# First attention of a hybrid block: sums alone in a group's first step, heads and outputs copied out of PSUM by ScalarE, the shared expert's gate and up apart, dense work in other steps

## The chip, the core and the metric

The kernel runs on one core of a Trainium2 chip. The metric is the device time of one execution in microseconds (us), from the runs of the kernel; lower is better. Five engines work side by side, each through its own queue in order: PE (TensorE, matmuls into PSUM), DVE (VectorE), ACT (ScalarE), POOL (GpSimd) and SP (SyncE, which issues most DMAs). They wait for each other through semaphores.

## The reference, cut to what matters

The program runs four layers over 16 sequences of 512 tokens of width 256, that is 8192 tokens: a softmax attention, a mixture of experts, an attention with forget gates, and the mixture of experts once more. The change touches the first attention and the part of the first mixture of experts that runs beside it.

```python
x = x + attn_a(layernorm(x))                     # 16 heads of 16, rope on q and k
x = x + ffn(layernorm(x))                        # 64 experts, top 8, and a shared expert
...
# attn_a
q, k, v = proj(Wq), proj(Wk), proj(Wv)
scores = einsum('bhqd,bhkd->bhqk', rope(q), rope(k)) / sqrt(16)
out = einsum('bhqk,bhkd->bhqd', softmax(scores), v)
return out.reshape(B, S, D) @ Wo.T
...
# shared expert, in ffn (192 wide)
gu = x @ ws_gate_up
shared = silu(gu[:, :192]) * gu[:, 192:] @ ws_down
```

## The kernel before, in words

All is in fp32. The first attention works in **blocks** of 512 tokens (one sequence, `nblk` = 16), each block in four **groups** of four heads, each group in four **steps** of 128 tokens. A block thus has 16 steps, and the loop over `s` runs from 32 steps ahead of block 0 to the end of block 15. The order of every engine's queue but POOL's is the order in which the loop calls the work (`manual_schedule`); `each(s)` yields it, so the tables in it are the schedule.

In a step, for group n and its i-th 128 tokens:

- `weighted(n, i)` (L364): four matmuls (L329, one per head, side by side on four row strips of PE) give the scores of 128 keys against 512 queries, and ACT takes four exponents (L369). `largest(n + 2, i)` (L338): four matmuls of the same kind (also L329) for the group two ahead, of which DVE takes the row maxima with four reduces (L343). The profile calls both L329; each matmul shows as two instructions. This is "L329" or "the scoring" in what follows.
- In step 0 of a group: `summed(n - 1)` (L373), 16 matmuls (L379, two instructions each) that sum the weighted values of the group before, copied out by ACT (L144); then `turn(n + 3)` of the keys (L312), four transposes (L318) and an ACT copy.
- In step 1: `heads(n - 1)` (L388, calls `heads_out`), four transposes (L152) of which DVE takes a reciprocal and a product straight from PSUM (L156, L160) into `ao`; `row(n + 1)` (L347), which brings the maxima into a row of the turned queries through PE, ACT (L359) and four SP DMAs (L362); then `turn(n + 3)` of the queries.

Behind that a step calls what the tables `dense` and `routed` (L423, L438) hold for its place in the block. The second number of an entry is how many blocks away the work belongs (`queries, 1` is for the next block, `output, -1` for the last one). `load`, `moments`, `normed`, `features` (L232 to L250) bring a block in, normalise it on DVE and turn it (L225); `queries` (L252, L255) projects queries and keys and leaves the rope to POOL; `values` (L295, L299); `joined` turns `ao` (L395); `output` (L398) multiplies by Wo (L402), and DVE adds it to `x` straight from PSUM (L409). `part.*` is the first mixture of experts, two or three blocks behind: `part.shared(b, piece)` runs the shared expert's up to three 128-wide chunks of gate and up (L1605) and its silu (tanh on ACT, L991, and two DVE products, L992 and L993, that read PSUM), `part.down` its second matmul (L1636); `part.moments`, `part.normed`, `part.features`, `part.logits`, `part.likely`, `part.exps`, `part.choose`, `part.count` and `part.added` make the router's tokens (L1516 turns them), logits (L1525), probabilities (L1537, L1539), choices and counts. `part.shared` and `part.down` are left out for the last blocks and done behind the loop.

Every matmul result takes one of eight PSUM banks, `bank()` (L214), in the order of the calls and in turn: a new result waits until whatever was read from the bank eight calls ago has been read. A step takes four banks for `weighted`, four for `largest`, and one for each further result (two for eight transposes).

Of the kernel before, what the change touches and what calls it, by code (L numbers as in the profile page):

```python
# [9 lines left out]
F32 = mybir.dt.float32  # L10
U32 = mybir.dt.uint32
AF = mybir.ActivationFunctionType
ALU = mybir.AluOpType
# [4 lines left out]
P = 128  # L18
D = 256
KD = D // P  # L20
H = 16
HD = D // H
HP = 32
NHG = 4
BLK = 512
# [12 lines left out]
class Block:  # L38
# [105 lines left out]
        self.nc.scalar.copy(oT, pav)  # L144
        return oT

    def heads_out(self, out, oT, hg, bank, den_eps=None):

        nc = self.nc
        pt = bank()  # L150
        for c in range(CB):
            nc.tensor.transpose(pt[:, ts(c, P)], oT[:, ts(c, P)], self.ident)  # L152
        o = pt.rearrange("p (c j k) -> p c j k", j=NHG, k=HP)
        rec = self.small.tile([P, CB, NHG], F32, name="rec")
        if den_eps is None:
            nc.vector.reciprocal(rec, o[:, :, :, HD])  # L156
        else:
            nc.vector.tensor_scalar(rec, o[:, :, :, HD], den_eps, None, ALU.add)
            nc.vector.reciprocal(rec, rec)
        nc.vector.tensor_tensor(  # L160
            out[:, :, ts(hg, NHG * HD)].rearrange("p c (j d) -> p c j d", d=HD),
            o[:, :, :, 0:HD],
            rec.unsqueeze(3).to_broadcast([P, CB, NHG, HD]),
            ALU.mult,
        )


    def attention(self, x, x1, wqkv, wo, rope, part, later):

# [9 lines left out]
        nc, tc = self.nc, self.tc  # L179
        with ExitStack() as c:  # L180
# [6 lines left out]
            p2 = c.enter_context(tc.tile_pool(name="a_2", bufs=2, side="left"))  # L187
# [200 lines left out]
            def heads(n):  # L388
                b, hg = divmod(n, NHG)
                if hg == 0:  # L390
                    aos[b] = p1.tile([P, CB, D], F32, name="ao")
                self.heads_out(aos[b], oTs.pop(n), hg, bank)


            def joined(b):  # L395
# [2 lines left out]
            def output(b, i):  # L398
                po = bank()
                for k in range(2):  # L400
                    for kd in range(KD):
                        nc.tensor.matmul(  # L402
                            po[:, ts(k, D)],
                            lhsT=aoTs[b][:, kd, ts(i + k, P)],
                            rhs=wo_sb[:, kd, :],
                            start=(kd == 0),
                            stop=(kd == KD - 1),
                        )
                nc.vector.tensor_tensor(  # L409
                    xs[b][:, i : i + 2, :],  # L410
                    xs[b][:, i : i + 2, :],
                    po.rearrange("p (c d) -> p c d", c=2),
                    ALU.add,
                )
# [6 lines left out]


            dense = {  # L423
                0: [(load, 2)],
                2: [(queries, 1, 2)],
                3: [(part.shared, -2, 1), (queries, 1, 3)],
                4: [(joined, -1)],
                6: [(values, 1, 0)],
                7: [(values, 1, 2)],
                8: [(moments, 2)],  # L430
                9: [(normed, 2)],
                10: [(output, -1, 0)],
                11: [(output, -1, 2)],
                13: [(features, 2)],
                14: [(queries, 2, 0)],
                15: [(queries, 2, 1)],
            }
            routed = {  # L438
                0: [(part.added, -3)],
                1: [(part.shared, -2, 0)],  # L440
                4: [(part.choose, -2, 0), (part.choose, -2, 1)],
                5: [(part.down, -2, 0), (part.choose, -2, 2)],
                9: [(part.down, -2, 2)],
                12: [(lambda b: part.moments(b, xs[b]), -1)],
                13: [(part.count, -2), (lambda b: part.normed(b, xs.pop(b)), -1)],
                14: [(part.features, -1)],
                15: [(part.logits, -1), (part.likely, -1), (part.exps, -1)],
            }
            steps, groups, z = NHG * CB, self.nblk * NHG, self.nblk - 1

            def each(s):

                n, i = divmod(s, CB)
                yield groups, n, weighted, i
                yield groups, n + 2, largest, i
                if i == 0:
                    yield groups, n - 1, summed
                    yield groups, n + 3, turn, kTs, H, "kT"
                if i == 1:
                    yield groups, n - 1, heads  # L460
                    yield groups, n + 1, row
                    yield groups, n + 3, turn, qTs, 0, "qT"
                b, at = divmod(s, steps)
                for work, far, *args in dense.get(at, []) + routed.get(at, []):

                    if b + far < z - 2 or work not in (part.shared, part.down):
                        yield self.nblk, b + far, work, *args

            with tc.manual_schedule(
                engines={  # L470
# [903 lines left out]
class Part:  # L1374
# [6 lines left out]
    def __init__(self, ctx, k, x, y, weights, room, pairs, side):  # L1381
# [21 lines left out]
            self.hTs,  # L1403
            self.ys,
            self.gus,
        ) = [{} for _ in range(12)]
        self.end = 0.0
        self.bank = None
        self.shared_weights = (rw, ws_gu, ws_down)
# [187 lines left out]


    def gu(self, b, piece):
        nc, xnT = self.nc, self.xnTs[b]  # L1600
        gu = self.gus[b, piece] = {}
        for m in ((0, 2), (1,))[piece]:
            gu[m] = self.bank()
            for kd in range(KD):
                nc.tensor.matmul(  # L1605
                    gu[m],
                    lhsT=self.wsg_sb[:, kd, ts(m, P)],
                    rhs=xnT[:, kd, :],
                    start=(kd == 0),
                    stop=(kd == KD - 1),  # L1610
                )
        if piece == 1:
            del self.xnTs[b]

    def silu(self, b, piece):
# [7 lines left out]
        self.k.silu(self.hTs[b][0:high, piece, :], gate, up, th, 0.5)  # L1623

    def shared(self, b, piece):
        self.gu(b, piece)
        self.silu(b, piece)
# [137 lines left out]
```

## Time and profile before

| | |
|---|---|
| median of 3 runs | 2688.24 us (2686.0 to 2689.28) |
| the profiled execution's own time | 2689.83 us |
| its span, first to last instruction | 2688.0 us |
| mean granted clock of PE | 0.953 |
| PE, DVE, ACT, POOL busy over the span | 91%, 71%, 48%, 31% |
| last heads of the first attention (L160, last start) | 1374.4 us |
| granted clock 107 to 119 and 119 to 125 us | 0.76 and 0.63 |
| granted clock 200 to 1200 us | 1.00 |
| granted clock 1299 to 1309 us | 0.56 |

How to read it: the span holds all four layers one after the other; what is said of one of them has to be read in its own stretch. Matmuls are pipelined and their ends are modelled, so PE's busy share says little; where a stretch of the chain of waits lies on PE from end to end, the length of each of its pieces is what counts, and a piece that is longer than its like elsewhere stood still on a wait.

### The profile page before, as it was taken

To read this page: it belongs to the slowest core of one execution; us is meant where nothing else is said; L and a number is where in the kernel's file an instruction comes from. 1 tells how busy PE (TensorE), PEld (TensorE's weight loads), DVE (VectorE), ACT (ScalarE), POOL (GpSimd) and SP (SyncE) were. 2 spreads that over 40 slices of the span, in tenths; PEclk is the share of its full clock that TensorE was granted. 3 is DMA by queue.
4 is the path that set the end of the run, shared out by engine and by line. 5 is a ranking of instruction groups with operands and counts; after the bars stand their busy time and mean duration, and the time that the engine had idled before them with its cause. 6 is when DMAs were issued, how large, how long until landed. Compare 5 with 4: busy or idle time off the path is not lost.

```text
span 2688.0 us, 47635 instructions
## 1 busy us (share of the span) xinstructions
PE 2447.6 (91%) x17864; PEld 1511.5 (56%) x17864; DVE 1895.4 (71%) x4646; ACT 1291.3 (48%) x2654; POOL 844.7 (31%) x804
## 2 busy tenths in 40 slices
PE   7999999999999999999988885899999969998781
PEld 3445455545455544555446775567667656667671
DVE  6666667666677666776646664899999869967650
ACT  1656556565566655665532332455555523323330
POOL 3122222122221222212015775332232122127773
PEclk7999999999999999999898998999999969999996
DMA  1000111001110001100158986201111058739987
GB/s 57 2 17 19 35 37 35 21 22 35 35 35 21 29 29 35 36 19 21 40 133 234 239 223 145 69 29 60 56 52 53 21 145 184 176 106 262 239 217 147
DMA packets 210003, 226.48 MB, mean 84 GB/s; under 512 B 34286, under 2 KB 202222, under 8 KB 208750
## 3 DMA queue, kind: packets, MB, share of 16 engines
q1 hardware_dynamic: 180366, 174.43, 22.5%
q0 software_dynamic: 25728, 46.15, 8.9%
q8 instruction: 143, 2.34, 0.4%
q10 hardware_dynamic: 3680, 2.85, 0.3%
q14 instruction: 86, 0.70, 0.1%
HBM read 146.50 MB, written 84.48 MB: 86 GB/s over the span
## 4 chain that ended last, share of the span: by engine, by line
PE 68%; DVE 15%; DMA 9%; issue 3%; POOL 1%; ACT 1%; SPq 0%; ACTq 0%; POOLq 0%; DVEq 0%
PE sc L329 20%; PE sc L379 9%; DMA xe<-rows,token 6%; PE sc L255 4%; DVE pT L841 4%; PE sc L1605 3%; PE sc L318 3%; DVE qkT L805 2%; PE sc L299 2%; PE sc L402 2%; PE sc L1636 2%; PE pb L792 2%; PE pb L717 2%; PE sc L1137 2%; PE sc L824 1%
## 5 line engine op out<-in xcount | busy, mean ns | idle before, releaser
L343 DVE TENSOR_REDUCE mx<-sc 128x1 f32<-128x512 f32 x1024 | 635.2, 682 | 375.7 <-PE sc L329 375.6
L369 ACT ACTIVATE pT<-sc 128x512 f32<-128x512 f32 x1024 | 528.6, 602 | 179.5 <-PE sc L329 179.5
L329 PE MATMUL sc<-qT,kT 17*128 17x512 f32 x2048 | 315.6, 646 | 0.0
L329 PE MATMUL sc<-kT,qT 16*128 16x512 f32 x2048 | 312.4, 609 | 1.5 <-DVE mx L343 1.4
L104 POOL TENSOR_SCALAR va<-mv 128x4 f32<-128x4 f32 x64 | 14.7, 230 | 797.1 <-DVE mv L98 797.1
L379 PE MATMUL sc<-pT,v 128*32 128x512 f32 x2048 | 241.8, 614 | 0.0
L329 PEld LDWEIGHTS sc<-kT,qT 16*128 16x128 f32 x2048 | 159.6, 189 | 94.4 <-issue 52.1
L841 DVE SCALAR_TENSOR_TENSOR pT<-sc,of,left 128x256 f32<-128x256 f32 x512 | 204.6, 472 | 4.3 <-PE sc L824 4.3
L277 POOL TENSOR_TENSOR t<-qk,rope_sb 128x512 f32<-128x512 f32 x62 | 78.8, 1270 | 403.4 <-ACT qk L263 396.6
L1107 POOL DMA_INDIRECT xe<-rows,token x128 | 128.5, 1004 | 96.2 <-DVE token L1089 39.0
L379 PEld LDWEIGHTS sc<-pT,v 128*32 128x32 f32 x2048 | 61.3, 112 | 173.1 <-issue 123.0
L329 PEld LDWEIGHTS sc<-qT,kT 17*128 17x128 f32 x2048 | 93.8, 184 | 89.9 <-issue 46.1
L255 PE MATMUL sc<-wqkv_sb,feat 128*128 128x512 f32 x256 | 127.4, 623 | 0.0
L144 ACT COPY oT<-sc 128x512 f32<-128x512 f32 x64 | 37.6, 587 | 169.4 <-PE sc L379 169.4
L792 PE MATMUL pb<-feat,wqk_sb 128*128 128x512 f32 x256 | 117.7, 593 | 0.0
L1172 POOL DMA_INDIRECT routed<-ye,token x64 | 105.0, 1641 | 39.1 <-DMA routed<-ye,token 16.2
L96 DVE BATCH_NORM_STATS2 bn<-x 128x6 f32<-128x256 f32 x256 | 89.0, 410 | 17.7 <-DMA x<-out 12.9
L318 PEld LDWEIGHTS sc<-ident,pad 128*128 128x128 f32 x512 | 54.8, 142 | 74.1 <-issue 38.9
L805 DVE SCALAR_TENSOR_TENSOR qkT<-ez,rz 128x512 f32<-128x512 f32 x64 | 93.9, 1487 | 0.0
L318 PE MATMUL sc<-ident,pad 128*128 128x128 f32 x512 | 86.1, 291 | 5.2 <-POOL pad L293 3.0
L285 POOL TENSOR_TENSOR t<-qk,rope_sb 128x256 f32<-128x256 f32 x124 | 90.7, 753 | 0.0
L1605 PE MATMUL sc<-xnT,wsg_sb 128*128 128x512 f32 x192 | 89.3, 603 | 0.0
(218 smaller groups left out, 4807.0 us busy)
## 6 DMA issues: line engine op xcount, KB each, us to landing
ws<-in_w_gate SPq DMA_DIRECT2D x64, 384.0 KB
ws<-in_w_up SPq DMA_DIRECT2D x64, 384.0 KB
rows<-xn SPq DMA_DIRECT2D x32, 512.0 KB
routed<-y SPq DMA_DIRECT2D x32, 512.0 KB
ws<-in_w_down SPq DMA_DIRECT2D x64, 256.0 KB
x<-in_x SPq DMA_DIRECT2D x16, 512.0 KB
attended<-x SPq DMA_DIRECT2D x16, 512.0 KB
ws<-in_w_down SPq DMA_DIRECT2D x64, 128.0 KB
```

The source lines that it names most:

```text
L255: nc.tensor.matmul(pq, lhsT=xnTs[b][:, kd, ts(i, P)], rhs=wqkv_sb[:, kd, 0 : 2 * D], start=(kd == 0), stop=(kd == KD - 1),)
L318: nc.tensor.transpose(pt[:, ts(i, P)], pads[b % 2][i][:, at : at + 4, :].rearrange("p h d -> p (h d)"), self.ident,)
L329: nc.tensor.matmul(scs[j], lhsT=lhs[at : at + high, ts(i, P)], rhs=rhs[at : at + high, :], start=True, stop=True,)
L343: nc.vector.tensor_reduce(mxs[n][:, j, i : i + 1], sc, AX.X, ALU.max, negate=True)
L369: nc.scalar.activation(pT[:, j, :], sc, AF.Exp, scale=float(HD) ** -0.5)
L379: nc.tensor.matmul(pav[ts(j, HP), :], lhsT=vs[b % 2][:, i, 4 * hg + j, :], rhs=pT[:, j, :], start=(i == 0), stop=(i == CB - 1),)
L792: nc.tensor.matmul(pq, lhsT=wqk_sb[:, kd, ts(m, P)], rhs=xnTs[b][:, kd, :], start=(kd == 0), stop=(kd == KD - 1),)
L805: nc.vector.scalar_tensor_tensor(qks[b][:, m, :], ez, 1.0, rz, ALU.min, ALU.add)
L841: nc.vector.scalar_tensor_tensor(pTs[n][:, :, ts(s8, HD)], sc[:, :, ts(s8, HD)], of[:, s8 : s8 + 1], here, ALU.mult, ALU.mult,)
L1107: nc.gpsimd.indirect_dma_start(out=xes[e], out_offset=None, in_=rows, in_offset=bass.IndirectOffsetOnAxis(ap=token[:, e : e + 1], axis=0),)
L1172: nc.gpsimd.indirect_dma_start(out=accs[e % 2], out_offset=bass.IndirectOffsetOnAxis(ap=token[:, e : e + 1], axis=0), in_=ye, in_offset=No ...
L1605: nc.tensor.matmul(gu[m], lhsT=self.wsg_sb[:, kd, ts(m, P)], rhs=xnT[:, kd, :], start=(kd == 0), stop=(kd == KD - 1),)
```

## The change

`heads_out` and `output` get a buffer `there`: ACT copies the PSUM result into it, and DVE works from there. The two tables become one, with its entries in other steps. `part.shared(-2, 0)`, which ran gate and up in one step, becomes `part.gate` (step 1) and `part.up` (step 3). In `each`, step 0 of a group calls the sums and no turn; the turn of the keys moves to step 1, ahead of the first dense entry, which itself comes ahead of `heads` and `row`; the turn of the queries moves to step 2. The copy in `heads_out` and `output` is also in what runs behind the loop.

```diff
-    def heads_out(self, out, oT, hg, bank, den_eps=None):
+    def heads_out(self, out, oT, hg, bank, pool, den_eps=None):
...
-        o = pt.rearrange("p (c j k) -> p c j k", j=NHG, k=HP)
+        there = pool.tile([P, BLK], F32, name="there")
+        nc.scalar.copy(there, pt)
+        o = there.rearrange("p (c j k) -> p c j k", j=NHG, k=HP)
...
-                self.heads_out(aos[b], oTs.pop(n), hg, bank)
+                self.heads_out(aos[b], oTs.pop(n), hg, bank, p2)
...
+                there = p2.tile([P, BLK], F32, name="there")
+                nc.scalar.copy(there, po)
                 nc.vector.tensor_tensor(
                     xs[b][:, i : i + 2, :],
                     xs[b][:, i : i + 2, :],
-                    po.rearrange("p (c d) -> p c d", c=2),
+                    there.rearrange("p (c d) -> p c d", c=2),
                     ALU.add,
                 )
...
             dense = {
-                0: [(load, 2)],
+                0: [(load, 2), (part.added, -3)],
+                1: [(part.gate, -2)],
                 2: [(queries, 1, 2)],
-                3: [(part.shared, -2, 1), (queries, 1, 3)],
-                4: [(joined, -1)],
-                6: [(values, 1, 0)],
-                7: [(values, 1, 2)],
+                3: [(part.up, -2), (queries, 1, 3)],
+                4: [(part.choose, -2, 0), (part.choose, -2, 1)],
+                5: [(part.shared, -2, 1), (joined, -1)],
+                6: [(values, 1, 0), (part.choose, -2, 2)],
+                7: [(part.down, -2, 0)],
                 8: [(moments, 2)],
-                9: [(normed, 2)],
-                10: [(output, -1, 0)],
-                11: [(output, -1, 2)],
-                13: [(features, 2)],
-                14: [(queries, 2, 0)],
-                15: [(queries, 2, 1)],
+                9: [(values, 1, 2), (normed, 2)],
+                10: [(output, -1, 0), (part.count, -2)],
+                11: [(features, 2), (output, -1, 2)],
+                12: [(lambda b: part.moments(b, xs[b]), -1)],
+                13: [(queries, 2, 0), (lambda b: part.normed(b, xs.pop(b)), -1)],
+                14: [(part.features, -1), (part.down, -2, 2)],
+                15: [(part.logits, -1), (part.likely, -1), (part.exps, -1), (queries, 2, 1)],
             }
-            routed = {
-                0: [(part.added, -3)],
-                1: [(part.shared, -2, 0)],
-                4: [(part.choose, -2, 0), (part.choose, -2, 1)],
-                5: [(part.down, -2, 0), (part.choose, -2, 2)],
-                9: [(part.down, -2, 2)],
-                12: [(lambda b: part.moments(b, xs[b]), -1)],
-                13: [(part.count, -2), (lambda b: part.normed(b, xs.pop(b)), -1)],
-                14: [(part.features, -1)],
-                15: [(part.logits, -1), (part.likely, -1), (part.exps, -1)],
-            }
+            expert = part.gate, part.up, part.shared, part.down
...
                 yield groups, n, weighted, i
                 yield groups, n + 2, largest, i
+                b, at = divmod(s, steps)
+                now = [
+                    (self.nblk, b + far, work, *args)
+                    for work, far, *args in dense[at]
+                    if b + far < z - 2 or work not in expert
+                ]
                 if i == 0:
                     yield groups, n - 1, summed
+                if i == 1:
                     yield groups, n + 3, turn, kTs, H, "kT"
-                if i == 1:
+                    yield from now[0:1]
                     yield groups, n - 1, heads
                     yield groups, n + 1, row
+                    now = now[1:]
+                if i == 2:
                     yield groups, n + 3, turn, qTs, 0, "qT"
-                b, at = divmod(s, steps)
-                for work, far, *args in dense.get(at, []) + routed.get(at, []):
-                    if b + far < z - 2 or work not in (part.shared, part.down):
-                        yield self.nblk, b + far, work, *args
+                yield from now
...
+    def gate(self, b):
+        gu = self.bank()
+        self.chunk(b, 0, gu)
+        self.hTs[b] = self.hidden[b % len(self.hidden)]
+        th = self.ths[b] = self.tile("th", [P, BLK])
+        self.nc.scalar.activation(th, gu, AF.Tanh, scale=0.5)
+        self.nc.vector.scalar_tensor_tensor(th, th, 1.0, gu, ALU.add, ALU.mult)
+
+    def up(self, b):
+        gu = self.bank()
+        self.chunk(b, 2, gu)
+        self.nc.vector.scalar_tensor_tensor(
+            self.hTs[b][:, 0, :], self.ths.pop(b), 0.5, gu, ALU.mult, ALU.mult
+        )
```

`chunk(b, m, to)` is the loop over two matmuls that `gu` had before, with the bank given to it.

More of the change, by code (lines that the diff above doesn't have):

```diff
@@ L1405, in __init__ @@
             self.gus,
-        ) = [{} for _ in range(12)]
+            self.ths,
+        ) = [{} for _ in range(13)]
         self.end = 0.0
@@ L1599, in gu @@
     def gu(self, b, piece):
-        nc, xnT = self.nc, self.xnTs[b]
         gu = self.gus[b, piece] = {}
@@ L1603, in gu, with chunk @@
             gu[m] = self.bank()
[L1604 to L1611, printed above, removed]
+            self.chunk(b, m, gu[m])
         if piece == 1:
             del self.xnTs[b]
+    def chunk(self, b, m, to):
+        for kd in range(KD):
+            self.nc.tensor.matmul(
+                to,
+                lhsT=self.wsg_sb[:, kd, ts(m, P)],
+                rhs=self.xnTs[b][:, kd, :],
+                start=(kd == 0),
+                stop=(kd == KD - 1),
+            )
     def silu(self, b, piece):
@@ L1623, in silu @@
         self.k.silu(self.hTs[b][0:high, piece, :], gate, up, th, 0.5)
+    def gate(self, b):
[10 more added lines that the diff above has]
+            self.hTs[b][:, 0, :], self.ths.pop(b), 0.5, gu, ALU.mult, ALU.mult
+        )
     def shared(self, b, piece):
```

## The prediction

> **What bounds the kernel now.** I read the page first, then the busy times of one block of the first attention, then the chain of waits there, then its timeline.
>
> ```profile
> PE 2447.6 (91%) x17864; PEld 1511.5 (56%) x17864; DVE 1895.4 (71%) x4646; ACT 1291.3 (48%) x2654; POOL 844.7 (31%) x804
> PE 68%; DVE 15%; DMA 9%; issue 3%; POOL 1%; ACT 1%; SPq 0%; ACTq 0%; POOLq 0%; DVEq 0%
> ```
>
> The whole kernel hangs mostly on PE, but that is an average over stages. The change touches only the stage up to about 1370 us (the last heads of the first attention). One of its blocks, by the view of stretches:
>
> ```profile
> 521.31:604.91 83.60, 83.60 (x562) 42.31 (x561) 57.96 (x129) 49.93 (x99) 19.63 (x22) 1.00 0.10 31
> ```
>
> A block lasts 83.60 us. PE's 83.60 means little, as ends of matmuls are modelled; what counts is that DVE (57.96) and ACT (49.93) have room, and that the chain there is PE alone. So only two things can be won: time in which PE's queue stands on a wait, and the cost of changing from one kind of matmul to another. Both show in the chain's pieces (start, length, what):
>
> ```profile
> 519.38 1.93 PE sc L329 x16
> 521.31 1.92 PE sc L402 x8
> 523.23 2.34 PE sc L329 x15
> 525.58 1.93 PE sc L402 x8
> ...
> 538.33 2.42 PE sc L329 x15
> 540.74 1.91 PE sc L255 x4
> ...
> 549.13 2.16 PE sc L329 x16
> 551.29 3.57 PE sc L379 x32
> 554.86 0.59 PE sc L318 x4
> ...
> 566.20 1.93 PE sc L329 x16
> 568.13 1.91 PE sc L1605 x4
> 570.05 1.72 PE sc L255 x4
> ```
>
> L329 is the scoring that opens every step, 1.93 us. Three of the sixteen in a block are longer: by 0.41 (step 11), 0.49 (step 14) and 0.23 (the next block's step 0). That is **1.13 us of waiting per block**. The last two lines show the other thing: four matmuls of 512 columns take 1.91 behind L329 and 1.72 behind matmuls of their own kind. Who is waited for, from the timeline:
>
> ```profile
> 523.73 0.68 DVE L409 TENSOR_TENSOR x<-x,sc 128x512 f32<-128x512 f32 x1
> 524.13 1.45 PE L329 MATMUL sc<-kT,qT 16*128 16x512 f32 x8
> ...
> 538.22 0.42 DVE L160 TENSOR_TENSOR ao<-sc,rec 128x256 f32<-128x256 f32 x1
> 538.26 1.20 PE L329 MATMUL sc<-qT,kT 17*128 17x512 f32 x7
> ```
>
> The eight PSUM banks are handed out in turn, so a step that takes d banks beyond its eight for L329 gives its positions d to d+7 to the next step's L329. DVE's add L409, queued behind four reduces, held the output's bank to 524.41; the second half of L329 (1.04 long elsewhere) took 1.45. L160 held the heads' bank to 538.64 likewise. The third, 0.23, is L1539, which reads the router's logits until 550.05.
>
> **The change, part by part, for a full block.** Times inside a step count from its L329's start: L329 ends at 1.93; ACT's four exponents run 1.2 to 3.3, DVE's four reduces 2.02 to 4.50, starting 0.60 apart (timeline: L329 at 519.31, L369 at 520.53, L343 at 521.33).
>
> *Copies out of PSUM.* Four heads and two outputs a block get an ACT copy, priced by the same copy in the second attention:
>
> ```profile
> L877 ACT COPY there<-pb 128x512 f32<-128x512 f32 x64 | 37.0, 578 | 0.3 <-PE pb L874 0.3
> L884 DVE TENSOR_TENSOR ao<-there,rec 128x256 f32<-128x256 f32 x64 | 27.2, 425 | 2.2
> L160 DVE TENSOR_TENSOR ao<-sc,rec 128x256 f32<-128x256 f32 x53 | 22.5, 424 | 1.8
> ```
>
> Six times 0.58 is 3.5 us of ACT; 49.9 becomes 53.4 of 83.6, hidden under PE. If ACT had no room it would be up to 3.5 a block. DVE's own time does not fall (425 against 424 ns), but the banks come free when ACT is done, 0.6 to 0.7 us behind PE, and no longer when DVE gets to them: the 0.41 and 0.49 go. [...]
>
> *Logits ahead of queries in step 15.* L1537 and L1539 then run right behind the reduces and end at about 5.3, a whole L329 before their bank is due (5.5 + 0.96): the 0.23 goes. All **1.13 is removed**.
>
> *Changes of kind.* Adding the chain's pieces (L329 1.93, sums 3.57, turn 0.59, heads 0.59, row 0.32, eight transposes 0.87, count 0.44, dense work 1.9 behind L329 and 1.72 to 1.80 behind others, logits 1.73) in the old order gives 82.4, with 1.13 of waits 83.55, which is the measured block. In the new order the steps come to: 0, 4, 8, 12 (sums alone) 5.50 each; 1, 5, 9, 13: 5.17, 6.04, 5.23, 5.15; 2, 6, 10, 14: 4.24, 4.32, 4.76, 5.19; 3, 7, 11, 15: 5.56, 3.85, 4.70, 5.48; together 81.7. So **0.73 less**, because eight dense pieces stood behind L329 and now four do. One change of kind is not in the trace: sums straight into L329. I give it the 0.1 that other changes cost (inside the 3.57). The nearest rows bound it: at nothing it saves another 0.4 a block; with a whole weight load of L329 uncovered on top (row of PEld: 185 ns) it costs 0.7 more.
>
> *New waits.* Here I walk the banks for each step; three places fail.
> (a) Step 5 takes six banks, so step 6's fourth L329 bank is that of the shared expert's third chunk. The chunk ends at 1.93 + 0.59 + 1.74 = 4.26, tanh (L991, 591 ns) starts 0.2 behind it as at 570.08 and ends at 5.05, DVE's L992 and L993 (680 and 690 ns) at 6.49; step 6 starts at 6.04: **0.45**.
> (b) Step 9: heads now stand behind a turn and the values. Their matmuls end at 4.9, their copy, behind that of the values, at 5.6; DVE's reciprocal starts there, and from it to the end of the normalising the old order took 2.58 (518.53 to 521.11): 8.2, that is 3.0 into step 10, where the reduces want DVE at 2.0. The third of them ends at 4.85 and its bank is due at 4.76: with a hand-over of 0.1, **0.2**.
> (c) Step 13 likewise: the router's normalised tokens are done, chunk by chunk, from 2.1 to 3.1 into step 14, where their transposes are due from 2.52 on: **0.4**. Before, queries stood between.
> Two others come within 0.1 (gate's bank in step 2, queries' in step 0); I add 0.05. New: **1.1**; each may be nothing, or twice that.
>
> The turns moved off step 0 are read two steps later, with their copy long done. The row's DMAs keep some 14 us to the next group, and SP's other issues (stores at steps 0, 6, 11, 13, 14) wait for nothing that would hold a row's. Heads of the first group now come ahead of "joined" on PE; the product waits for it on DVE, and DVE is then still at L993: nothing.
>
> *Sum.* 0.73 + 1.13 − 1.1 = 0.76 a block; 12 full blocks (2 to 13): **−9.1**. Blocks 0 and 1 lack the dense work of older blocks; L329 stretches to 11.44 for three steps at 107 us, and the sums behind it take 5.95 in place of 3.57 at a granted clock of 0.63 (119 to 125 us). Values and features now lie among these steps: **−3**, bounds 0 and −6. In block 15 (1299 to 1309 us, clock 0.56) work is missing in both orders: 0, bounds ±4. [...] Behind the loop, the last heads and the second output each get a copy in a chain that nothing covers (heads' product 1374.43, outputs 1378.36 and 1379.56): **+1.2**. The DMA-bound experts behind only shift. In all −10.9 against the profiled 2689.83 (span 2688.0); that execution lies 1.6 above the runs' median of 2688.24, so I forecast **2677**.
>
> **Rivals.** 1, *the new waits take all* (each of (a) to (c) 0.25 larger, or the sums' change of kind with its uncovered load): 0.0 to 0.1 a block, 2685 to 2688. For it: three waits went, three came. Against: the removed ones are measured, the new ones reckoned with latencies at their high end.
> 2, *DVE runs late, slower than before.* In steps 9 and 13 the queue copy, heads, normalising, reduces is serial; every us that the heads' copy comes later than 5.6 delays reduces and transposes at both places. From 0.4 us at each the gain of a block is gone; at 1.1 us each it costs 2.2 − 0.76 = 1.4 a block, 17 us, less 2 at the ends: 2703. For it: DVE already has 58 of 84 us, and its queue is in order. Against: ACT is free at that point (its turn's copy ends at 3.9).
> 3, *the new waits do not arise*: 1.9 a block, 22 us, with the ends 2664.
> 4, *no difference at all*, as PE is busy 83.60 of 83.60: 2688. Against: the three longer L329.
>
> **How the numbers follow.** Forecast 0.40, rival 3 0.16, rival 1 (with 4) 0.24, rival 2 0.20. A measurement here tells about 0.2% (5.4 us) from no change. Faster takes the forecast and rival 3: 0.56; the same 0.24; slower 0.20. The range runs from rival 3 with the half clocks gone (2661) to where half of rival 2 lies inside (2698). The forecast's own range is 2670 to 2683.
>
> **What would show it.** In the new profile a full block should last 82.8 us. No L329 is long behind an output or heads; those of steps 6 and 11 are long by 0.45 and 0.2, waiting for the shared expert's last product and for a reduce; the router's transposes in step 14 take 1.3 in place of 0.87. L329 right behind sums stays at 1.93. I am wrong if the block is over 83.6, or if L343 in steps 10 and 14 starts over 3.5 into its step.

## The result, and the profile after

The changed kernel takes **2717.74 us** (median of 4 runs, 2711.4 to 2720.38); the kernel before, beside it on the same chip, 2687.12 (4 runs, 2680.82 to 2689.28). The ratio is 1.0114, 95% interval 1.0088 to 1.014: 30 us slower, where 11 faster was forecast. The profiled execution took 2720.38, with a span of 2718.2.

The lines of code move a little: scoring is L334 (was L329), its reduces L348 (L343), sums L384, turn L323, queries L260, the rope's three lines L282, L290 and L298, the router's transposes L1523, its logits L1532, the shared expert's gate and up L1617, its second matmul L1662 ("down" below). New is L154, the heads' copy; behind it come L158 and L162, reciprocal and product.

Busy times and the shares of the chain of waits, from the page of the changed kernel:

```profile
PE 2454.6 (90%) x17864; PEld 1528.9 (56%) x17864; DVE 1930.3 (71%) x4646; ACT 1335.3 (49%) x2750; POOL 847.6 (31%) x804
PE 67%; DVE 17%; DMA 9%; issue 3%; ACT 1%; POOL 1%; SPq 0%; ACTq 0%; POOLq 0%; DVEq 0%
```

ACT has the 96 copies more. DVE issues exactly as many instructions as before (x4646) and yet is busy 35 us longer: some of the same instructions take more time. One block, by the view of stretches (length, busy time of PE, PEld, DVE, ACT, POOL, then the granted clock):

```profile
482.88:568.21 85.33, 83.36 (x565) 43.10 (x564) 60.58 (x129) 52.84 (x105) 19.83 (x22) 0.98 0.10 29
```

The block lasts 85.33 us, not 83.60 as before or 82.8 as forecast. PE is no longer busy from end to end, the granted clock is below 1.00, and DVE is busy 2.6 us longer with its 129 instructions. The chain of waits shows where (step 13 begins at 548.47, step 14 at 553.39, step 15 at 562.58; the last line is step 6 of the next block):

```profile
538.12 2.10 PE sc L334 x16
...
548.47 1.93 PE sc L334 x16
550.40 0.58 PE sc L323 x4
550.98 1.73 PE sc L260 x4
...
553.30 0.58 ACT there L154
...
553.90 0.26 DVE rec L158
...
554.19 0.81 DVE ao L162
555.00 0.63 DVE t L113
...
555.66 0.67 DVE t L114
...
556.55 1.26 DVE xn L122
557.81 0.14 issue
557.94 2.21 PE sc L1523 x8
560.15 2.43 PE sc L1662 x8
562.58 1.93 PE sc L334 x16
...
600.07 1.93 PE sc L334 x16
```

The pieces on PE have the lengths that their like have elsewhere, but for step 14 and 0.17 in step 11 (538.12). There the chain leaves PE: the router's transposes (L1523) wait for the normalising, and most of the DVE operations ahead of it are long. The product takes 0.81 (0.42 before), the two operations on 128 x 4 numbers 0.63 and 0.67 (0.15 and 0.16 before), the first normalised chunk 1.26 (0.41 before); together they are some 2.25 us longer. These are the short ones, in the timeline of before (the product's 0.42 stands in the prediction):

```profile
538.56 0.15 DVE L113 SCALAR_TENSOR_TENSOR t<-y 128x4 f32<-128x4 f32 x1
538.75 0.16 DVE L114 TENSOR_TENSOR t<-t,va 128x4 f32<-128x4 f32 x1
...
539.14 1.38 DVE L122 TENSOR_SCALAR xn<-x,mv,rstd 128x256 f32<-128x256 f32 x4
```

The timeline of the changed kernel shows what else runs:

```profile
553.46 1.26 POOL L282 TENSOR_TENSOR t<-qk,rope_sb 128x512 f32<-128x512 f32 x1 [3.03 <-ACT qk L268]
...
553.90 0.25 DVE L158 RECIPROCAL rec<-there 128x16 f32<-128x16 f32 x1 [1.00 <-ACT there L154]
...
554.19 0.81 DVE L162 TENSOR_TENSOR ao<-there,rec 128x256 f32<-128x256 f32 x1
...
554.68 1.62 POOL L290 TENSOR_TENSOR t<-qk,rope_sb 128x256 f32<-128x256 f32 x2
554.92 0.70 DVE L113 SCALAR_TENSOR_TENSOR t<-y 128x4 f32<-128x4 f32 x1
...
555.66 0.66 DVE L114 TENSOR_TENSOR t<-t,va 128x4 f32<-128x4 f32 x1
556.35 0.16 DVE L116 SCALAR_TENSOR_TENSOR rstd<-t,y 128x4 f32<-128x4 f32 x1
556.38 1.27 POOL L298 TENSOR_TENSOR pad<-t,t 128x512 f32<-128x512 f32 x1
...
556.55 2.21 DVE L122 TENSOR_SCALAR xn<-x,mv,rstd 128x256 f32<-128x256 f32 x4
...
557.94 2.21 PE L1523 MATMUL sc<-ident,xn 128*128 128x128 f32 x8 [1.97 <-DVE xn L122]
```

POOL's rope of the moved queries has four operations, ending at 554.72, 555.60, 556.30 and 557.64. The four long DVE operations end at 555.00, 555.62, 556.32 and 557.80: each 0.02 to 0.28 behind the end of one on POOL. L116 starts just before the last of them and takes its 0.16; the three chunks after the rope take 0.40 each. Not everything in SBUF was held: the reciprocal (L158), which reads one tensor, ran beside the first rope operation in the 0.25 that it takes elsewhere.

So PE stands: from the start of its last matmul ahead (555.70) to the start of the first transpose (557.94) are 2.24 us, 1.97 of them idle. All lengths of a stand below are such times from start to start. It is followed by a half clock (the clock granted to PE is 0.5 of full speed), in the view of stretches:

```profile
555.40:558.00 2.60, 0.64 (x5) 0.42 (x5) 2.50 (x5) 1.69 (x4) 2.17 (x3) 1.00 0.01 2
558.00:560.10 2.10, 2.10 (x9) 1.70 (x10) 2.10 (x6) 0.58 (x1) 0.00 (x0) 0.51 0.18 62
560.10:562.60 2.50, 2.50 (x13) 1.82 (x11) 1.06 (x2) 0.58 (x1) 0.00 (x0) 0.73 0.46 157
```

In the first 2.6 us PE is busy for 0.64; then transposes and down run at a lower clock (2.21 and 2.43; where e11 has the same stand and a full clock behind it, they take 1.65 and 1.73). By the records of the clock in the trace, each full block has one stretch of half clock, 3.41 us long; before, none had one.

**Where the 30 us are**, by the copies of the sums at the ends of blocks: 4.3 up to the end of block 0, 8.0 in block 1, 20.5 in the 12 full blocks (1.73 in most), −6.6 and +0.2 in the last two, +4.0 behind the loop. The granted clock goes with the parts outside the full blocks, here of before and then of the changed kernel:

```profile
150.00:235.00 85.00, 85.00 (x559) 41.17 (x559) 55.03 (x114) 50.45 (x100) 20.70 (x23) 1.00 0.07 20
...
1290.00:1380.00 90.00, 88.42 (x523) 42.32 (x522) 47.02 (x121) 47.38 (x95) 5.89 (x12) 0.85 0.26 72
```

```profile
150.00:235.00 85.00, 83.03 (x526) 42.05 (x525) 52.74 (x106) 49.31 (x99) 18.48 (x20) 0.90 0.06 20
...
1290.00:1380.00 90.00, 89.86 (x638) 44.66 (x641) 57.11 (x125) 59.49 (x121) 5.37 (x9) 0.98 0.21 66
```

Block 1 (150 to 235 us) has the same stand, and half clock for 17 of these 85 us, by an estimate (half of the 17) worth up to 8.5: enough for the 8.0 lost there, though the two are not separated. In the last blocks the clock is better than before, which goes the way of the 6.6 gained (not tested by itself).

### The profile page after: what moved, and what is told of

It reads as the page before. It is cut to its first block, busy times and chain, and to the rows that moved or that the text cites. A ratio compares the mean times of both kernels' runs of the same rounds, so it can differ in the third digit from the quotient of the medians.

```text
span 2718.2 us, 47672 instructions
## 1 busy us (share of the span) xinstructions
PE 2454.6 (90%) x17864; PEld 1528.9 (56%) x17864; DVE 1930.3 (71%) x4646; ACT 1335.3 (49%) x2750; POOL 847.6 (31%) x804
## 4 chain that ended last, share of the span: by engine, by line
PE 67%; DVE 17%; DMA 9%; issue 3%; ACT 1%; POOL 1%; SPq 0%; ACTq 0%; POOLq 0%; DVEq 0%
PE sc L334 18%; PE sc L384 9%; DMA xe<-rows,token 5%; PE sc L260 4%; DVE pT L847 4%; PE sc L1617 3%; PE sc L323 3%; PE sc L1662 3%; DVE qkT L811 2%; PE sc L407 2%; PE sc L304 2%; PE pb L798 2%; PE sc L1143 2%; PE pb L723 2%; PE pb L1143 2%
## 5 line engine op out<-in xcount | busy, mean ns | idle before, releaser
L348 DVE TENSOR_REDUCE mx<-sc 128x1 f32<-128x512 f32 x1024 | 635.5, 683 | 336.9 <-PE sc L334 336.8
L334 PE MATMUL sc<-qT,kT 17*128 17x512 f32 x2048 | 312.2, 647 | 0.0
L334 PE MATMUL sc<-kT,qT 16*128 16x512 f32 x2048 | 293.2, 604 | 0.3 <-DVE mx L348 0.3
L384 PE MATMUL sc<-pT,v 128*32 128x512 f32 x2048 | 242.2, 615 | 0.1
L282 POOL TENSOR_TENSOR t<-qk,rope_sb 128x512 f32<-128x512 f32 x62 | 78.6, 1268 | 429.1 <-ACT qk L268 422.0
L334 PEld LDWEIGHTS sc<-kT,qT 16*128 16x128 f32 x2048 | 150.2, 189 | 84.2 <-issue 30.9
L334 PEld LDWEIGHTS sc<-qT,kT 17*128 17x128 f32 x2048 | 92.2, 184 | 130.7 <-issue 108.7
L384 PEld LDWEIGHTS sc<-pT,v 128*32 128x32 f32 x2048 | 61.4, 112 | 172.0 <-issue 122.6
L260 PE MATMUL sc<-wqkv_sb,feat 128*128 128x512 f32 x256 | 126.8, 621 | 0.0
L323 PEld LDWEIGHTS sc<-ident,pad 128*128 128x128 f32 x512 | 55.4, 144 | 104.7 <-ACT pT L374 81.1
L1577 POOL TENSOR_TENSOR wt<-pr,chosen 128x256 f32<-128x256 f32 x32 | 23.2, 725 | 241.5 <-DVE chosen L1572 217.1
L290 POOL TENSOR_TENSOR t<-qk,rope_sb 128x256 f32<-128x256 f32 x124 | 93.2, 772 | 0.0
L323 PE MATMUL sc<-ident,pad 128*128 128x128 f32 x512 | 87.0, 293 | 5.1 <-POOL pad L298 3.0
```

Of the source, the lines that this page charges most:

```text
L260: nc.tensor.matmul(pq, lhsT=xnTs[b][:, kd, ts(i, P)], rhs=wqkv_sb[:, kd, 0 : 2 * D], start=(kd == 0), stop=(kd == KD - 1),)
L323: nc.tensor.transpose(pt[:, ts(i, P)], pads[b % 2][i][:, at : at + 4, :].rearrange("p h d -> p (h d)"), self.ident,)
L334: nc.tensor.matmul(scs[j], lhsT=lhs[at : at + high, ts(i, P)], rhs=rhs[at : at + high, :], start=True, stop=True,)
L348: nc.vector.tensor_reduce(mxs[n][:, j, i : i + 1], sc, AX.X, ALU.max, negate=True)
L384: nc.tensor.matmul(pav[ts(j, HP), :], lhsT=vs[b % 2][:, i, 4 * hg + j, :], rhs=pT[:, j, :], start=(i == 0), stop=(i == CB - 1),)
```

## The experiments

Theories: **P**, POOL's rope, moved into step 13, holds DVE's operations; **L**, the chain on DVE is late in itself, as in rival 2; **C**, the copies make it late. All comparisons are with the kernel before on the same chip (medians 2685.33, 2686.06, 2683.23 and 2686.37 in the four groups of runs). "Block" is the length of a full block in the profiled execution.

| kernel | us | ratio to before, 95% | block |
|---|---|---|---|
| e1 rope later | 2664.01 | 0.9921 (0.9894 to 0.9949) | 81.71 |
| e2 no rope | 2672.93 | 0.9958 (0.9944 to 0.9971) | 81.72 |
| e3 from PSUM | 2724.96 | 1.0152 (1.0123 to 1.018) | 85.6 to 87.3 |
| e4 down first | 2757.91 | 1.0274 (1.0245 to 1.0303) | 88.75 |
| e5 copies alone | 2677.99 | 0.9965 (0.9949 to 0.998) | 82.85 |
| e6 move alone | 2728.94 | 1.0155 (1.0127 to 1.0183) | seven of 85.03, five of 86.7 to 91.4 |
| e7 queries first | 2662.96 | 0.992 (0.9894 to 0.9946) | 81.68 |
| e8 normed first | 2658.93 | 0.9902 (0.9882 to 0.9922) | 81.58 |
| e9 both first | 2659.41 | 0.9904 (0.9879 to 0.9929) | 81.65 |
| e10 later, from PSUM | 2666.3 | 0.9939 (0.9916 to 0.9961) | 82.12 |
| e11 after, more work | 2733.4 | 1.0159 (1.0127 to 1.019) | 84.93 to 87.55 |
| e12 later, more work | 2679.54 | 0.9966 (0.9954 to 0.9978) | 82.60 |

**e1: the rope later.** Two entries of the changed kernel's table change places:

```diff
-                13: [(queries, 2, 0), (lambda b: part.normed(b, xs.pop(b)), -1)],
-                14: [(part.features, -1), (part.down, -2, 2)],
+                13: [(part.down, -2, 2), (lambda b: part.normed(b, xs.pop(b)), -1)],
+                14: [(part.features, -1), (queries, 2, 0)],
```

> In the changed kernel a full block lasts 85.33 us; in step 14 the router's transposes wait 2.13 us for the normalised tokens and then run at half pace (some 1.8 us more with the matmuls behind them). Here the projection with its rope and one half of the shared expert's second matmul change places between steps 13 and 14, so heads still stand behind a dense piece of the same length, but POOL has no rope while DVE normalises. Theory P (POOL's rope holds DVE's instructions that read two operands from SBUF): from reciprocal to the end of normalising takes 2.6 us again, a wait of 0.5 at most, block 81.6 to 82.2, execution 2660 to 2675. Theory L (the chain copy, heads, normalising, reduces is late in itself because heads stand behind a dense piece): the wait stays, block 85.3, 2718. Theory C (the copies out of PSUM are what makes it late): 85.3, 2718.

Measured: 2664.01, block 81.71, no half clock in the full blocks. DVE's part of the timeline, from the end of step 13 on:

```profile
618.50 0.25 DVE L158 RECIPROCAL rec<-there 128x16 f32<-128x16 f32 x1 [0.96 <-ACT there L154]
618.79 0.43 DVE L162 TENSOR_TENSOR ao<-there,rec 128x256 f32<-128x256 f32 x1
619.13 0.16 DVE L113 SCALAR_TENSOR_TENSOR t<-y 128x4 f32<-128x4 f32 x1
619.32 0.16 DVE L114 TENSOR_TENSOR t<-t,va 128x4 f32<-128x4 f32 x1
...
619.72 1.38 DVE L122 TENSOR_SCALAR xn<-x,mv,rstd 128x256 f32<-128x256 f32 x4
```

The same operations, in the same order behind the same copy, at their short durations. The transposes take 1.28, the 0.4 of waiting that the prediction gave them. One exchange of two entries turns 30 us lost into 21 won; L and C, which leave the rope out of account, fall.

**e2: no rope.** To see that it is POOL and not the place of queries or down on PE, the changed kernel leaves out the rope of the first 128 tokens of every block but the first (ACT copies the projection in its place), with every entry where the change put it:

```diff
+                if b > 0 and i == 0:
+                    nc.scalar.copy(
+                        pads[b % 2][i][:, :, 0:HD], pq.rearrange("p (h d) -> p h d", d=HD)
+                    )
+                    return
```

> The changed kernel in which the rope of the first 128 tokens of every block but the first is left out (ACT copies the projection from PSUM into its place, POOL does nothing for it); the order of PE, DVE and SP is the changed kernel's. P: normalising takes 2.6 us from the reciprocal on, the wait in step 14 is 0.5 at most, block 81.6 to 82.2, execution 2660 to 2675. L and C: nothing changes on DVE, block 85.3, execution 2718.

Measured: 2672.93, block 81.72, transposes 1.28, the product 0.42, no half clock in the full blocks. P again. That the whole gains less than e1 lies at the ends: block 1 lasts 81.3 and the last one 67.6, against 77.6 and 58.4.

**e3: from PSUM.** The changed kernel with both copies undone:

```diff
-        there = pool.tile([P, BLK], F32, name="there")
-        nc.scalar.copy(there, pt)
-        o = there.rearrange("p (c j k) -> p c j k", j=NHG, k=HP)
+        o = pt.rearrange("p (c j k) -> p c j k", j=NHG, k=HP)
```

> The changed order with both copies out of PSUM undone: DVE reads heads and outputs from PSUM again. P: the reciprocal starts 0.6 earlier and the product reads one operand from SBUF only, but the three small instructions and the normalising still meet the rope; the wait in step 14 shrinks by 0.5 to 1.3, while 0.3 to 0.5 of waits for banks come back; block 84.3 to 85.5, execution 2705 to 2722. C: the wait goes, block about 82, 2670. L: the wait shrinks by the 0.6 of the copy, block 84.5.

Measured: 2724.96, as slow as the change or slower, and above the 2705 to 2722 that P gave it: the copies are not the cause. Its timeline holds a comparison that nothing else gives:

```profile
555.66 1.27 POOL L280 TENSOR_TENSOR t<-qk,rope_sb 128x512 f32<-128x512 f32 x1 [3.03 <-ACT qk L266]
555.67 0.42 DVE L160 TENSOR_TENSOR ao<-sc,rec 128x256 f32<-128x256 f32 x1
556.01 0.93 DVE L113 SCALAR_TENSOR_TENSOR t<-y 128x4 f32<-128x4 f32 x1
556.88 1.44 POOL L288 TENSOR_TENSOR t<-qk,rope_sb 128x256 f32<-128x256 f32 x2
556.98 0.66 DVE L114 TENSOR_TENSOR t<-t,va 128x4 f32<-128x4 f32 x1
```

The product, one of whose operands now lies in PSUM, runs wholly beside a rope operation and takes 0.42; with both in SBUF it took 0.81. The small operation behind it, with all its inputs in SBUF, takes until that rope operation ends.

**e4: down first.** Only the order within step 14 changes, so that PE has down to do while the normalising runs:

```diff
-                14: [(part.features, -1), (part.down, -2, 2)],
+                14: [(part.down, -2, 2), (part.features, -1)],
```

> The changed kernel with the two entries of step 14 exchanged: the shared expert's second matmul (1.8 us) stands ahead of the router's transposes. DVE and POOL keep their order. P and L alike: the tokens are as late as before (5.4 us into step 14), but PE has work until 4.3, so the wait is 0.3 to 1.0 and, if the half pace comes from PE's standing still, it is gone; block 82.0 to 83.0, execution 2670 to 2690. If the half pace stays without the long wait, block about 84. P shows in the profile: the product still 0.8, the small ones 0.7 each; L would have them at 0.42 and 0.16.

A miss, and a clear one: 2757.91, block 88.75. PE's stand ahead of the transposes did fall, from 2.24 us to 0.63, with DVE's operations as long as in the changed kernel (0.82, 0.63, 0.67, 1.26), but the wait moved on: DVE's reduces stand behind the late normalising, and step 15's scoring waits for them and for their banks. The chain there, and the clock:

```profile
568.47 1.64 PE sc L1523 x8
570.11 5.40 PE sc L334 x15
575.51 3.60 PE sc L1532 x16
579.12 3.07 PE sc L260 x4
```

```profile
570.10:575.50 5.40, 5.40 (x18) 2.20 (x17) 3.19 (x6) 3.07 (x6) 0.00 (x0) 0.62 0.93 291
575.50:582.20 6.70, 6.70 (x25) 4.61 (x24) 1.72 (x4) 0.42 (x1) 0.00 (x0) 0.54 0.01 2
```

Three stretches of half clock in a row, 10.24 us, where the changed kernel has one. My expectation covered one consumer of the late engine and forgot the next.

**e5: the copies alone**, in the kernel before:

```diff
-        o = pt.rearrange("p (c j k) -> p c j k", j=NHG, k=HP)
+        there = pool.tile([P, BLK], F32, name="there")
+        nc.scalar.copy(there, pt)
+        o = there.rearrange("p (c j k) -> p c j k", j=NHG, k=HP)
```

> The kernel before with only the two copies by ScalarE added (heads and outputs), in the old order. Theory P (the loss of the whole change is GpSimd's rope holding DVE): in the old order no rope runs beside the heads' product, so the copies show what they were priced at: the two waits of 0.41 (step 11) and 0.49 (step 14) go, a block lasts 82.7 in place of 83.6 us, and with 1.2 us more behind the loop the time is 2675 us, 10 below the kernel before (2668 to 2681). The heads' product stays at 0.42 us. Rival C (the copies are what costs): the block is as before or longer, 2685 to 2700, with the product of step 13 over 0.6 us or its normalising late.

Measured: 2677.99, block 82.85, product 0.42. Step 11's wait is gone (1.93), step 14's fell from 0.49 to 0.14: 0.76 of the 0.90 that the prediction gave them.

**e6: the move alone**, in the kernel before, without copies:

```diff
-                11: [(output, -1, 2)],
-                13: [(features, 2)],
-                14: [(queries, 2, 0)],
+                11: [(output, -1, 2), (features, 2)],
+                13: [(queries, 2, 0)],
```

> The kernel before, without copies, with two entries of its table moved: the features of the block two ahead from step 13 to step 11, and the projection of queries from step 14 to step 13, where it comes ahead of the router's normalising. Theory P: the rope then starts about 6.0 us after step 13's start, when DVE is just behind the heads' product; the normalising needs some 5.3 us from there, as in the changed kernel, in place of 2; it ends about 5.5 us into step 14, where the router's transposes now want it at 1.9, so they wait 2.5 to 3 us: a block of 86 to 88 us, 2715 to 2740. Its small operations (0.16 each) and first normalised chunk (0.41) are long, ending just behind a rope operation each; the heads' product, which reads PSUM, stays at 0.42. Rival L (the chain is late in itself, no matter what GpSimd does): the normalising ends 2.3 into step 14 as before, the transposes wait 0.3 to 0.4, step 14's scoring wait of 0.49 goes or stays: a block of 83.2 to 84.0, 2680 to 2690, and the small operations stay at 0.16.

Measured: 2728.94, as P said; seven blocks of 85.03 (a little under my 86 to 88) and five longer ones, those with half clock. My detail missed: the small operations were done before the rope began. It met the normalised chunks instead, which took 0.41, 1.48, 0.83 and 0.83:

```profile
558.81 3.31 DVE L122 TENSOR_SCALAR xn<-x,mv,rstd 128x256 f32<-128x256 f32 x4
...
559.20 1.27 POOL L277 TENSOR_TENSOR t<-qk,rope_sb 128x512 f32<-128x512 f32 x1 [4.57 <-ACT qk L263]
...
560.43 1.54 POOL L285 TENSOR_TENSOR t<-qk,rope_sb 128x256 f32<-128x256 f32 x2
...
562.04 1.27 POOL L293 TENSOR_TENSOR pad<-t,t 128x512 f32<-128x512 f32 x1
```

So neither the copies nor the new order of step 0 and 1 is needed for the loss; moving the queries, with the features that they read, does it. The reduces, which read PSUM, lie beside the last rope operation and keep their 0.68.

**e7: queries first**, e1 with step 14's entries exchanged:

```diff
-                14: [(part.features, -1), (queries, 2, 0)],
+                14: [(queries, 2, 0), (part.features, -1)],
```

> The kernel with the rope put later (step 13 with the second matmul of the shared expert, step 14 with features and then queries; block 81.71 us), with one more exchange: in step 14 the projection of queries comes ahead of the router's features. The transposes are then due 1.7 us later and the 0.41 us for which they wait (1.28 in place of 0.87) go: block 81.3 us, 5 us less in all, 2659 us (2653 to 2666). By P nothing else changes, since the rope then starts some 4 us into step 14, behind the normalising, beside reduces that read PSUM: small operations 0.16, chunks 0.41. If instead reduces are held by the rope too, the step behind gets longer and the block is at 81.7 or more, 2664 and above.

Half a miss: the transposes fell to 0.87, but the block only to 81.68. The 0.4 reappears as 0.37 in the next scoring (2.30), which waits for the last of step 14's reduces. The wait was never PE's order; it is DVE being late.

**e8: the normalising first**, e1 with step 13's entries exchanged:

```diff
-                13: [(part.down, -2, 2), (lambda b: part.normed(b, xs.pop(b)), -1)],
+                13: [(lambda b: part.normed(b, xs.pop(b)), -1), (part.down, -2, 2)],
```

> The kernel with the rope put later (block 81.71 us; step 13: second matmul of the shared expert, then the router's normalising), with the two entries of step 13 exchanged, so that the normalising comes ahead of the heads in DVE's queue and the second matmul behind them in PE's. What is left there is DVE standing for 0.96 us on ScalarE's copy of the heads with the normalising queued behind (the wait that the prediction called (c)). If that is all of it, DVE goes from its reduces straight into the normalising, ends it 1.2 us earlier, at 1.4 into step 14, the transposes are 0.87 in place of 1.28, and the next reduces start at 2.0 to 2.2 in place of 2.9; heads and down change kind once more, which costs 0.15 to 0.25: a block of 81.4 to 81.5, 3 us less in all than that kernel, 2661 (2655 to 2667). If the heads' product, now later, delays something (its buffer, the attention's output matmul in step 5 and behind), the block is over 81.7.

Measured: 2658.93, block 81.58. Transposes 0.87 and the next scoring 1.93, so the 0.41 goes; changes of kind give 0.28 back (down 1.93 in place of 1.73, queries 1.80 in place of 1.72). The fastest median of the study, though its interval overlaps e1's.

**e9: both first**, e8 with step 9's entries exchanged too:

```diff
-                9: [(values, 1, 2), (normed, 2)],
+                9: [(normed, 2), (values, 1, 2)],
```

> As the last kernel, and in step 9 too the normalising ahead of the heads (and the values behind them). The wait of step 11 that the prediction called (b), measured 0.15 to 0.17 there, should go, as the reduces of step 10 then start on time; one more change of kind takes about as much back: a block equal to the last kernel's within 0.1 us. If (b) came from something else than DVE's late normalising, the scoring of step 11 stays at 2.08.

Measured: 2659.41, block 81.65. Step 11's scoring is 1.93 (2.10 in the changed kernel), the values behind it 1.92 in place of 1.73: as expected, even.

**e10: e1 without the copies** (the edit of e3 in e1).

> The kernel with the rope put later, without the two copies by ScalarE (heads and outputs read from PSUM by DVE): what the copies are worth where nothing holds DVE. By the bank waits that the copies removed in the old order (0.75 of 0.90 measured there) and the two that came back with the same undoing in the changed kernel (step 2's scoring 2.46, step 6's 2.27): block 82.4 to 82.7 in place of 81.71, 2671 (2665 to 2678). If the copies are worth nothing, or cost ScalarE time that counts, 2664 or less.

Measured: 2666.3, block 82.12, with waits in step 2 (2.46) and step 6 (2.28). The copies are worth 0.41 a block here, less than I expected, since without them DVE need not wait for ACT and the transposes take 0.92 in place of 1.28; the intervals of the two times overlap.

**e11 and e12: more work for PE.** The blocks of the changed kernel and of e4 settle at 85.33 and 88.75 us, 25 and 26 times 3.413. Do the half clocks make room for added work? The heads' transposes are done twice in two of the four groups, in the changed kernel and in e1:

```diff
-        for c in range(CB):
+        for c in [*range(CB)] * (2 if hg in (0, 3) else 1):
             nc.tensor.transpose(pt[:, ts(c, P)], oT[:, ts(c, P)], self.ident)
```

> The changed kernel with work added that nobody needs: the four transposes of the heads are done twice (into the same bank) for two of the four groups, those whose heads fall in steps 1 and 5; PE gets eight more transposes a block, 0.11 us each, 0.88 us, and 0.9 to 1.0 with the rest of the chain. In the changed kernel a block settles at 85.33 us, which is 25 times the 3.413 us that its one stretch of half clock lasts; with the down matmul first it was 88.75, 26 times. Theory G (the half clock comes and goes on a fixed grid of 3.413 us, and the blocks fall into step with it): at full clock the block is some 83.5 us, the rest is filled by as much of the half clock as falls on work; added work then takes the place of half clock, the block stays at 85.33 (85.28 to 85.38) and the time within 3 us of the changed kernel's, 2715 to 2721. Theory S (a stand of a given length costs a given half clock behind it, and all costs add up): the block is 86.2 to 86.4, 10 to 12 us more in all, 2728 or so.

> The same added work in the kernel with the rope put later, whose blocks (81.71 us) hold no half clock. Both theories: nothing can give way, the block is 82.6 to 82.7 and the time 10 to 12 us above that kernel's 2664, 2675 (2670 to 2680). If the block stays at 81.7, the added transposes are hidden anyway and the other run tells nothing.

e12 went as expected (82.60, 0.89 more a block). In e11 neither theory holds: the blocks go from 84.93 to 87.55 in turn, with no half clock, one stretch of 3.41 or two (6.83) behind a stand that is 2.24 us long each time. In its blocks without a half clock the transposes wait only for their chunks, and down runs at full pace:

```profile
994.72 1.65 PE sc L1523 x8
996.36 1.73 PE sc L1662 x8
```

That separates the two costs: 84.93 less 0.87 of added work (heads 0.87 in place of 0.44, twice) is 84.06, so what the rope does to DVE costs 84.06 − 81.71 = 2.35 a block, and the half clock behind it 85.33 − 84.06 = 1.27 more in the changed kernel.

Which of the blocks of e11 get a half clock, the records of the clock tell. Every stretch of it begins on a grid of 3.413 us. In the ten full blocks that have one, 1.47 to 2.25 us of the stand lie ahead of a step of the grid, and the half clock begins at that step; in the two that have none, the step divides the stand into 1.06 and 1.18 us (step at 300.76) and into 1.19 and 1.05 (993.67). In the 12 full blocks of the changed kernel 2.06 or more lie ahead of the step, in those of e3 1.45 or more, and all have a half clock. So in these three kernels the half clock goes with the part of the stand between two steps: none at 1.19 us or less, always at 1.45 or more.

## Why the prediction was wrong

**The step that failed is (c)**: "Step 13 likewise: the router's normalised tokens are done, chunk by chunk, from 2.1 to 3.1 into step 14". They were done from 4.4 to 5.4 in, the reduces started 5.3 in (the text named 3.5 as the bound beyond which it is wrong), and the term of 0.4 became 0.4 + 2.35 + 1.27 = 4.0. The chain was reckoned with durations of the old order, as in (b): "from it to the end of the normalising the old order took 2.58", where no rope lay beside it. I had taken into account what the moved queries do on PE and ACT, but not that the four operations of their rope follow on POOL as soon as ACT has copied them. Nothing was missing from the trace of before: the rope's place and length were in it, and so were DVE's operands. It did not show the two together, and such a cost should have been bounded: by an estimate, at worst DVE waits out the whole rope, some 4 us (its four operations lie between 209.00 and 213.01 there).

What I did not weigh is where the inputs of DVE's operations lie. Beside the moved rope the product took 0.81 with two SBUF inputs against 0.42 with one in PSUM (e3), and the operation on 128 x 4 numbers that takes 0.15 elsewhere took 0.63 and longer; the ends of the four long operations lie 0.02 to 0.28 behind POOL's ends. The reciprocal, with one SBUF input, was not held (0.25). How POOL holds them the traces do not show, and they leave one point open: the chunks, with one SBUF tensor and two per-partition scalars, were held too (1.26 in place of 0.41).

The other steps:

- *Removed waits, 1.13*: right. All three are gone in the changed kernel; the copies' two came to 0.76 of 0.90 alone (e5).
- *Changes of kind, 0.73*: right in kind, too small. e1's 81.71 less its two waits (0.41, 0.17) is 81.13, not 81.7; four heads at 0.44 behind dense work in place of 0.59 are those 0.6. Sums straight into the scoring stay at 3.57 and 1.93, as taken.
- *(a), 0.45*: did not come; step 6's scoring is 1.93. The third chunk's last product (L999) does run until 515.04, 0.29 into step 6, but the first matmuls of all four heads of that scoring have started by 514.71, so none of them writes the chunk's bank. At this place, then, the banks are not handed out in turn by the order of the calls, as the prediction and the text ahead of it have it; how they are handed out is open.
- *(b), 0.2*: right, 0.17 (2.10 in place of 1.93), and of the cause given, as e9 shows.
- *Copies hidden under PE*: right; with ACT's 3.5 us more a block, e5 is 0.75 a block shorter than before, and e1 0.41 shorter than e10.
- *Ends*: −3 for blocks 0 and 1 became +12.2. Block 1's 8.0 goes back with e1 (77.6 as before). The 4.3 up to the end of block 0 do not go back (5.6 in e1, 1.3 in e9), and what is behind the loop lies between 1307 and 1319 us in these kernels: both stay open.

**Rival 2** had the place right, DVE's serial chain in step 13, and the sign, but not the reason. It argued against itself that ACT is free; the engine to look at was POOL. It asked for 1.1 at two places; 2.35 came at one, and the half clock behind it, 1.27 a block or 15 us, was priced by no rival.

Without step 13's collision the forecast's kind of gain is there: e1 is 21 us faster than before, more than the 11 forecast, since (a) did not come and the heads were cheaper.

## What to carry to other kernels

When an instruction is moved, follow all that it sets off on the other engines to the time at which that will run, and look at what runs there now: a duration is known only beside the neighbours with which it was measured (the product took 0.42 alone and 0.81 beside the rope). For DVE beside POOL, list the inputs: what read a tensor from PSUM was free of it here (product 0.42 in e3, reduces 0.68), and so was the reciprocal of one SBUF tensor (0.25); what had two inputs in SBUF was not (0.81), nor were the normalised chunks (1.26 in place of 0.41). And mind that a stand of the matmul engine can cost more than its length: here half clock followed the stand of 2.24 us and cost 1.27 us more a block.

## What the runs showed of the hardware

- DVE operations with two inputs in SBUF that ran beside one of the rope's on POOL ended 0.02 to 0.28 us behind it (the changed kernel), small ones too (0.15 became 0.63 to 0.93); one that started 0.02 ahead of POOL's kept its 0.16 (L116). With one of the two in PSUM the product took its 0.42 (e3). The reduces from PSUM (0.68) and the reciprocal of one SBUF tensor (0.25) were not held; the chunks, of one SBUF tensor and two per-partition scalars, were (0.41 became 0.83 to 1.48).
- The half clock has a grid. In each of the 14 traces, every stretch of it between 200 and 1400 us is 3.41, 6.83, 10.24 or 13.65 us long, and all of one trace begin at the same phase of 3.413 us, within 0.01. In the full blocks of the changed kernel, e3 and e11, 1.45 us or more of a stand between two steps of the grid was followed by half clock each time, 1.19 or less was not. In e6 no two matmuls start over 1.1 us apart in the full blocks, and five of the twelve have a half clock; what sets it off there is not shown. Two kernels fell into step with the grid (25 and 26 of its units a block) and e11 did not; why is open.
